# First placing in halves, the last sequence's halves side by side, and the clearing transfers three in a row behind the maxima's

## The chip, the cores and the metric

The kernel runs on one core of one Trainium2 chip. The metric is the device time of one execution in microseconds (us); less is better. TensorE (PE) multiplies matrices and loads its weights (PEld), VectorE (DVE), ScalarE (ACT) and GpSimd (POOL) work on tiles, and SyncE (SP) does little but begin DMA transfers. ACT and POOL begin some as well. Each engine takes its instructions in the order in which the program gives them; engines wait for each other with semaphores.

## The reference

The input is x, 16 sequences of 256 tokens with 128 features. Three blocks follow one another: a plain attention, and two layers of attention and a mixture of experts.

```python
x = x + layernorm(attn(layernorm(x)))          # 16 heads of 8, causal
h = x                                           # the sandwich: 2 layers
for l in range(2):
    h = h + attn(ln1(h), wq[l], wk[l], wv[l], wo[l])     # 16 heads of 8, causal
    moe = token_moe if l == 0 else seq_moe
    h = h + moe(ln2(h), ...)                    # 8 experts, 128 -> 512 -> 128, the best 2
x = x + layernorm(h)

def token_moe(h):   # each token goes to its own two experts
    cw = weights of the two largest of (h @ gw + gb), softmax over them
    return sum_e (gelu(h @ w1[e] + b1[e]) @ w2[e] + b2[e]) * cw[..., e]
def seq_moe(h):     # the two experts are chosen once per sequence, by the mean over its tokens
    ...
```

## The kernel before, in words

**A written order.** The kernel is a list of steps: `plan.put(slot, fn, phase)` notes a step, and at the end all are sorted by slot, phase (EARLY, MAIN, LATE) and order of noting, and written out (`Plan`, L352). Nothing is rearranged afterwards, so the order in a slot is the order in every engine's queue. A sequence of the attentions takes `NT` = 6 slots. Slots below 0 are the start. The plain attention has slots 0 to 95, layer 0's attention the 96 after it; layer 1's comes after the experts of layer 0.

**An attention.** Sequences go in pairs. `plan_pair` normalizes both, transposes them (`to_hT`, ACT L648) and projects q and k for all heads into PSUM (`project`, tile pp, L403). The values are split in a high part (`high`, ACT L410) and a low one (`low`, DVE L415), both in one tile hl, which has a single buffer, for q and k together. `place(k, n)` (L424) moves hl into the rows that TensorE reads: eight transfers of 256 KB for a pair, four for each sequence, from 128 partitions of hl to every eighth partition of `qk_rows[i + k]`. There are four such row tiles in turn. Their fixed rows are set once by `clear` (L169), a cast over half of the tile; the two casts of tile 0 stand at the head of ACT's queue, and those of tile 1 at slot -14. All placings are begun on SP but for two of each sequence of the first pair, which ACT begins.

`plan_sequence` then makes scores twice. A first pass (L299, with the causal mask by L276) finds the maxima of each row (DVE, mx). They are transposed, split in high and low (`high_max`, `low_max`) and sent to two more rows of qk_rows as mhi and mlo (SP, L508) at slot 3 of each group of six, EARLY. The second pass (L320) computes the scores less their maxima in the product itself, and ACT takes the exponential (pT, L324). L339 weights the values. The result is brought into order by small transfers on SP: sums and y (L522, L523), inv and r (L528, L534). POOL multiplies (y, L541), PE projects (po, L546). In the plain attention, POOL adds the input xr, which SP has loaded again (an, L636), and SP stores the sum (x, L637).

**The order on SP.** In the slots of a pair whose placings are due it is: mhi, mlo, store of x, four placings, inv, a clearing transfer, four placings, loads of xr (and for some pairs x), a clearing transfer, two r, sums, y, a clearing transfer. In the other half of the pair's twelve slots there are no placings: mhi, mlo, store of x, inv, clearing transfer, xr, clearing transfer, two r, sums, y, clearing transfer.

**Clearing.** Layer 0's experts read their tokens from x_rows, sorted by expert, and leave results in y_rows; both are DRAM arrays with room for incomplete tiles. SP writes zeros over them first, in 88 transfers of 256 KB from one zero tile (L1307), one at every even slot: 68 for x_rows, 20 for y_rows.

**Experts of layer 0.** POOL scatters the tokens' rows to x_rows (L883); tiles of 256 rows go through `plan_tokens` and their results to y_rows (`store` of a tile, POOL L1176). Tokens come in two parts, `q` = 0 and 1. Layer 1 begins with gathers (POOL L756), two for each block of 128 tokens, which must follow the stores that they read. The gathers of sequence 0 carry dependences on the stores noted so far, up to `NA_T + NB_T`. The store of the last of them (q = 1, m = `NB_T - 1` = 13) is written after the first two gathers.

**The end.** In layer 1 a sequence's expert products are added to z (L1237 and after), normalized and added to x. For the last sequence, `halves` does it for 128 tokens at a time: add (L1254), statistics, root on POOL (L248, L249), scaling and the last addition on DVE (L253, L1262), and the store on SP or ACT (L1265). Other sequences have `store` (L1288): POOL adds and then begins the output's transfer (L1290).

Of the kernel before, what the change touches and what calls it, by code (L numbers as in the profile page):

```python
# [75 lines left out]
def sandwich_kernel(  # L76
# [107 lines left out]

    nc.scalar.activation(hs[:, 0:1], nhalf[:, 0:1], AF.Exp)
    clear(nc.scalar.copy, 0, 0)
    clear(nc.scalar.copy, 0, 1)
    ones = const.tile([P, P], F32, name="ones")
    before = const.tile([P, P], F32, name="before")
    euler = const.tile([P, 1], F32, name="euler")  # L190
# [2 lines left out]
    def start_steps(plan):  # L193


        def loads():
            for b in range(2, 4):
                x0[b] = load_x(b, "x0", 6)
            nc.sync.dma_start(row, rows.partition_broadcast(P))
            nc.scalar.dma_start(wvo_sb[:, 0], wvo[0])  # L200

        def late_loads():
            for a in range(1, 3):
                nc.scalar.dma_start(wqk_sb[:, a], wqk[a])
                nc.scalar.dma_start(wvo_sb[:, a], wvo[a])
            nc.scalar.dma_start(gw_sb, gw)

        def rest():
            nc.gpsimd.memset(ones, 1.0)
            nc.gpsimd.affine_select(  # L210
                out=before, in_=ones, compare_op=ALU.is_gt, fill=0.0, base=0, pattern=[[1, P]],
                channel_multiplier=-1,
            )
            nc.gpsimd.memset(euler, math.e)
            nc.gpsimd.memset(zeros, 0.0)

        plan.put(-34, loads)
        plan.put(-14, lambda: clear(nc.scalar.copy, 1, 0), MAIN)
        plan.put(-14, lambda: clear(nc.vector.tensor_copy, 1, 1), MAIN)
        plan.put(-31, lambda: make_mask(0))  # L220
        plan.put(-31, make_pick)
        plan.put(-16, lambda: make_mask(1))
        plan.put(-34, late_loads)
        plan.put(-15, lambda: make_va(va[0]))
        for i in range(2, 4):
            for h in range(2):
                slot = (-8 + 2 * h, -4)[i - 2]
                plan.put(slot, lambda i=i, h=h: clear(nc.scalar.copy, i, h))
        plan.put(-8, lambda: make_va(va[1]))
        plan.put(-8, rest)  # L230
# [148 lines left out]
    def plan_pair(plan, i, a, sources, applied, hT_of, done=None):  # L379
# [40 lines left out]
        def place(k, n):  # L420

            q, kk = n // 2, 2 + n % 2
            eng = nc.scalar if i == 0 and n > 1 else nc.sync
            eng.dma_start(  # L424
                qk_rows[(i + k) % NQ][n : P : 8].bitcast(F32),
                st["hl"][:, q : kk + 1 : kk - q, k],
            )

        def values():
# [41 lines left out]
        plan.put(t, lambda: high(0), EARLY)  # L471
        plan.put(t, lambda: low(0))
        for n in range(4):
            plan.put(t + (n // 2 if i else 0), lambda n=n: place(0, n), (LATE, EARLY)[n // 2 if i else 0])
            plan.put(t + 2 + n // 2, lambda n=n: place(1, n), (LATE, EARLY)[n // 2])
        plan.put(s0 - 2, values)
        plan.put(s0 - 1, to_va, EARLY)
# [270 lines left out]
    def plan_combine(plan, s, b, pace, adds):  # L748


        st = {}

        def gather(i):
            if i == 0:
                st["y"] = work.tile([P, 4, D], F32, tag="yg", name=f"yg_{b}")
            get = nc.gpsimd.indirect_dma_start(  # L756
                st["y"][:, i], None, y_rows,
                bass.IndirectOffsetOnAxis(ap=ix_y[:, 2 * b + i // 2, i % 2 : i % 2 + 1], axis=0),
            ).ins

            if i == 0 and b in (0, BA):
                for store in stores[: NA_T + NB_T] if b == 0 else stores[NA_T + NB_T :]:
                    tc.add_manual_dep(get, store.name, SYNC)
            apart_from(get, "y")

        def add(i):
            zt = z[b][:, i // 2]
            nc.vector.scalar_tensor_tensor(
                zt, st["y"][:, i], w_tok2[:, 2 * b + i // 2, i % 2 : i % 2 + 1], zt,
                ALU.mult, ALU.add,  # L770
            )

        for i in range(4):
            plan.put(s + i // pace, lambda i=i: gather(i))
            plan.put(adds[i // 2], lambda i=i: add(i))
# [338 lines left out]
    def plan_tokens(plan, s, q):  # L1114

        x_blocks = x_rows.rearrange("(c i p) d -> c p i d", i=2, p=P)
        y_blocks = y_rows.rearrange("(c i p) d -> c p i d", i=2, p=P)
        spare = {}

        def room(m):  # L1120


            if m == 2:
                parts = work.tile([P, 8, 2, D], F32, tag="hl", name="x_hl", bufs=1)
                spare.update({2 + i: parts[:, i] for i in range(8)})
            if m == 10:
                parts = work.tile([P, 4, D], F32, tag="yg", name="x_yg")
                spare.update({m + i: parts[:, 2 * i : 2 * i + 2] for i in range(2)})
            if m == 12:
                spare[m] = work.tile([P, 4, D], F32, tag="xn", name="x_xn", bufs=1)[:, 0:2]  # L1130
            return spare.get(m)

        def unit(m):
            tag = f"t{q}_{m}"

            st = {}

            def fetch():
                if q:
                    load()  # L1140
                return nc.sync.value_load(ix_tile[q][0:1, m, 0:1], min_val=0, max_val=E - 1)

            def load():
                eng = nc.sync if q else nc.gpsimd
                c = eng.value_load(ix_tile[q][0:1, m, 1:2], min_val=0, max_val=BLOCKS - 1)
                st["xt"] = room(m) if q == 0 else None
                if st["xt"] is None:
                    st["xt"] = work.tile([P, 2, D], F32, tag="xr", name=f"xt_{tag}", bufs=2)
                get = eng.dma_start(st["xt"], x_blocks[bass.ds(c, 1)].squeeze(0)).ins
                for put in puts[seen[0] :]:  # L1150
                    tc.add_manual_dep(get, put.name, SYNC)
                seen[0] = len(puts)

            if q == 0:
                plan.put(s - 5 + m // 2, load, MAIN)

            def turn():

                st["pt"] = transposed(
                    [st["xt"][:, i] for i in range(2)], tag, "p" if q == 0 or m < NB_T else "m"  # L1160
                )

            def affine():
                st["h"] = work.tile([P, T], F32, tag="r", name=f"ht_{tag}")
                nc.scalar.activation(  # L1165
                    st["h"], st["pt"], AF.Identity,
                    bias=vec[:, C_LN2B : C_LN2B + 1], scale=vec[:, C_LN2W : C_LN2W + 1],
                )

            def done(po, b2):  # L1170
                y = work.tile([P, 2, D], F32, tag="ao", name=f"y_{tag}")
                nc.vector.tensor_tensor(y, po, b2.unsqueeze(1).to_broadcast([P, 2, D]), ALU.add)  # L1172
                st["y"] = y

            def store():
                store = nc.gpsimd.dma_start(y_blocks[NA_T * q + m], st["y"]).ins  # L1176
                stores.append(store)
                apart_from(store, "y")

            plan_expert(plan, s + 2 * m, tag, w_tok, fetch, lambda: st["h"], done)  # L1180
            plan.put(s + 2 * m + 5, store, EARLY)
            plan.put(s + 2 * m - 1, turn, MAIN)
            plan.put(s + 2 * m, affine, EARLY)

        for m in range(TILES_OF[q]):
            unit(m)
# [36 lines left out]
    def plan_seq(plan, s):  # L1223

        for b in range(B):
# [3 lines left out]
            def unit(b, k):  # L1229
# [19 lines left out]
                def halves(pos, b2):  # L1249

                    o = work.tile([P, 2, D], F32, tag="an", name="o_last")
                    for i, po in enumerate(pos):
                        zi = z[b][:, i : i + 1]
                        nc.vector.scalar_tensor_tensor(  # L1254
                            zi, po, we[:, b, k : k + 1], zi, ALU.mult, ALU.add
                        )
                        mv = moments(2, f"last_{i}")[:, 0:1]
                        stats(mv, zi, f"last_{i}")
                        rs = small.tile([P, 2], F32, tag="rs2", name=f"rs_last_{i}")[:, 0:1]
                        root(rs, mv)  # L1260
                        scaled(nc.vector, o[:, i : i + 1], zi, mv, rs)
                        nc.vector.tensor_tensor(  # L1262
                            o[:, i : i + 1], o[:, i : i + 1], out_st["x"][:, i : i + 1], ALU.add
                        )
# [22 lines left out]

            def store(b=b, st=out_st):  # L1288
                nc.gpsimd.tensor_tensor(st["o"], st["o"], st["x"], ALU.add)  # L1289
                nc.gpsimd.dma_start(out[b].rearrange("(i p) d -> p i d", p=P), st["o"])  # L1290

            t = s + 4 * b + 6
            plan.put(t - 4, load)
# [6 lines left out]
    start_steps(plan)  # L1300
    attention_0(plan)

    n = 0
    for t in (x_rows, y_rows):
        fill = t.rearrange("(c p r) d -> c p (r d)", p=P, r=4)
        for c in range(fill.shape[0]):
            plan.put(2 * n, lambda fill=fill, c=c: nc.sync.dma_start(fill[c], zeros))  # L1307
            n += 1
    layer_attention(plan, 0, B, finish_tok)

# [77 lines left out]
```

## Time and profile before

| what | value |
|---|---|
| time, three runs | 1017.8, 1020.77, 1027.81 us; median 1020.77 |
| profiled execution, its own time | 1017.52 us |
| its span (first to last instruction or transfer) | 1015.5 us |
| mean granted TensorE clock | 0.964 of full |
| busy: PE / DVE / ACT / POOL | 923.1 / 674.6 / 568.0 / 610.9 us |
| DMA moved | 163.64 MB, mean 161 GB/s |
| clearing transfers begun | x_rows from 43.6 to 350.7 us, y_rows from 353.1 to 440.8 us |

In a line of the profile, L is the line of the kernel, "a<-b" the written and the read tile, and the bracket at the end says how long the engine had stood idle before the instruction, and what ended that, as far as the semaphores tell. "SPq", "ACTq" lines are the beginnings of transfers. The list of waits sums such idle times: us in total, times, longest. The profile is of one execution, and sums are made against its own time.

### The profile page before, as it was taken

What the parts mean: (1) busy time and instruction counts of PE and PEld (TensorE: products, weight loads), DVE (VectorE), ACT (ScalarE), POOL (GpSimd) and SP (SyncE); (2) the same over time, 40 slices, a digit from 0 to 9 for tenths busy, and PEclk for the clock granted to TensorE, in tenths of its full rate; (3) what the DMA queues carried; (4) which work ended last, traced back from release to release, by engine and by line L of the source; (5) the groups of instructions that cost most, each with busy time, mean ns of one, the idle gap of its engine ahead of it and who ended that gap; (6) DMA issues with size and microseconds to landing.
All of it is one profiled execution on the core that took longest, in us unless ns stands there. A gap on an engine that the chain in (4) does not pass through costs nothing. (4 is left out here: it accounts for less than half of the span.)

```text
span 1015.5 us, 29356 instructions
## 1 busy us (share of the span) xinstructions
PE 923.1 (91%) x11148; PEld 721.6 (71%) x11148; DVE 674.6 (66%) x1614; ACT 568.0 (56%) x903; POOL 610.9 (60%) x1028
## 2 busy tenths in 40 slices
PE   3799889999999999998889999889999999999996
PEld 1566666666667777775788898766676677689996
DVE  3668778888788888885433413468899988445433
ACT  3565556666566666565344555345666666754442
POOL 7114666667766477658675127658688643366655
PEclk8799999999999999998799999899999999999999
DMA  6657677777877765542656787935565556256773
GB/s 162 136 121 174 169 179 188 182 188 192 191 178 173 170 168 155 166 132 71 198 166 190 218 235 235 242 91 119 125 128 116 106 113 144 67 151 197 203 202 106
DMA packets 143900, 163.64 MB, mean 161 GB/s; under 512 B 26928, under 2 KB 109872, under 8 KB 143760
## 3 DMA queue, kind: packets, MB, share of 16 engines
q1 hardware_dynamic: 133920, 142.41, 57.2%
q0 software_dynamic: 7312, 17.18, 5.6%
q10 hardware_dynamic: 2528, 2.18, 1.0%
q8 instruction: 88, 1.44, 0.6%
q14 instruction: 52, 0.43, 0.1%
HBM read 65.38 MB, written 37.36 MB: 101 GB/s over the span
## 5 line engine op out<-in xcount | busy, mean ns | idle before, releaser
L302 DVE TENSOR_REDUCE mx<-s 128x4 f32<-128x1024 f32 (+1 forms) x288 | 350.6, 1218 | 94.2 <-PE s L299 89.8
L324 ACT ACTIVATE pT<-s 128x1024 f32<-128x1024 f32 x288 | 294.4, 1023 | 164.4 <-PE s L320 160.3
L276 PEld LDWEIGHTS <-pick 64*128 64x128 bf16 x2304 | 78.1, 95 | 144.6 <-issue 122.1
L299 PE MATMUL s<-qk_rows 62*128 62x128 f32 (+1 forms) x1536 | 160.4, 306 | 11.0 <-DMA qk_rows<-hl 11.0
L320 PE MATMUL s<-qk_rows 64*128 64x128 f32 (+1 forms) x1536 | 158.4, 305 | 9.1 <-DMA qk_rows<-mlo 9.1
L339 PE MATMUL av<-pT,va 128*32 128x256 f32 (+1 forms) x3072 | 156.3, 333 | 0.0
L299 PEld LDWEIGHTS s<-qk_rows 62*128 62x128 f32 x1536 | 114.2, 194 | 13.6 <-issue 11.6
L320 PEld LDWEIGHTS s<-qk_rows 64*128 64x128 f32 x1536 | 112.3, 193 | 12.9 <-DMA qk_rows<-mhi 11.6
L276 PE MATMUL s<-mask_q,pick 64*128 64x128 bf16 (+1 forms) x1152 | 95.0, 243 | 18.8 <-DVE mx L302 14.5
L1083 ACT ACTIVATE gs_t<-ph_t,w_t 128x256 f32<-128x256 f32 x156 | 65.3, 470 | 71.5 <-PE ph_t L1079 67.0
L276 PE MATMUL s<-mask_k,pick 64*128 64x128 bf16 (+1 forms) x1152 | 94.2, 242 | 11.6 <-ACT pT L324 9.4
L339 PEld LDWEIGHTS av<-pT,va 128*32 128x32 f32 x3072 | 79.7, 110 | 33.3 <-issue 1.1
L1083 ACT ACTIVATE gs_s<-ph_s,w_s 128x256 f32<-128x256 f32 x128 | 52.7, 470 | 59.4 <-issue 57.3
L1093 PE MATMUL pe_t<-w_t,gs_t 128*128 128x128 f32 x624 | 80.4, 284 | 2.1 <-DVE y_t L1172 2.1
L1079 PE MATMUL ph_t<-ht_t,w_t 128*128 128x256 f32 x312 | 79.2, 398 | 1.7 <-ACT ht_t L1165 1.2
L883 POOL DMA_INDIRECT x_rows<-zn,ix_tok x64 | 65.1, 1017 | 25.5 <-issue 14.8
L1093 PEld LDWEIGHTS pe_t<-w_t,gs_t 128*128 128x128 f32 x624 | 76.2, 199 | 3.5 <-DVE y_t L1172 2.6
L756 POOL DMA_INDIRECT yg<-y_rows,ix_y x64 | 64.3, 1004 | 13.0 <-issue 12.7
L1172 DVE TENSOR_TENSOR y_t<-pe_t,w_t 128x256 f32<-128x256 f32 x39 | 16.5, 422 | 81.0 <-PE pe_t L1093 72.7
L1079 PEld LDWEIGHTS ph_t<-ht_t,w_t 128*128 128x128 f32 x312 | 58.7, 199 | 10.9 <-DVE mx L302 1.6
L1176 POOL DMA_DIRECT2D y_rows<-y_t x39 | 28.9, 742 | 60.6 <-DVE y_t L1172 48.4
L1093 PE MATMUL pe_s<-w_s,gs_s 128*128 128x128 f32 x512 | 62.8, 276 | 0.6 <-issue 0.6
(205 smaller groups left out, 1505.8 us busy)
## 6 DMA issues: line engine op xcount, KB each, us to landing
qk_rows<-hl SPq DMA_DIRECT2D x188, 256.0 KB
x_rows<-zeros SPq DMA_DIRECT2D x68, 256.0 KB
w_t<-in_w_tok SPq DMA_DIRECT2D x39, 320.0 KB
w_s<-in_w_seq SPq DMA_DIRECT2D x32, 320.0 KB
w_t<-in_w_tok SPq DMA_DIRECT2D x39, 258.0 KB
w_s<-in_w_seq SPq DMA_DIRECT2D x32, 258.0 KB
y<-at SPq DMA_DIRECT2D x48, 128.0 KB
r<-inv SPq DMA_DIRECT2D x96, 64.0 KB
```

The costliest lines, as they stand in the source:

```text
L276: nc.tensor.matmul(s[:, a, :, o + 64 * c : o + 64 * c + 64], pick[h, c], masks[m][h, 0:nj], start=(c == 0), stop=False, skip_group_check=True,
L299: nc.tensor.matmul(s[:, a, j], qs, ks, start=False, stop=(j == nj - 1), skip_group_check=True)
L302: nc.vector.tensor_reduce(mx[:, 0 if u is None else 1, :, j0 : j0 + nj], s, AX.X, ALU.max)
L320: nc.tensor.matmul(s[:, a, j], ks, qs, start=False, stop=(j == nj - 1), skip_group_check=True)
L324: nc.scalar.activation(pT, sc, AF.Exp, scale=SCALE)
L339: nc.tensor.matmul(o[:, P:] if u is None else o, v[:, i, 8 * par + 4 * a + jj % 4], p[:, a, j], start=(c not in first), stop=False, skip_g ...
L756: get = nc.gpsimd.indirect_dma_start(st["y"][:, i], None, y_rows, bass.IndirectOffsetOnAxis(ap=ix_y[:, 2 * b + i // 2, i % 2 : i % 2 + 1], ...
L883: put = nc.gpsimd.indirect_dma_start(x_rows, bass.IndirectOffsetOnAxis(ap=ix_tok[:, 4 * g + i, k : k + 1], axis=0), zns[2 * g + i // 2][:, ...
L1079: nc.tensor.matmul(p, w1[:, f * P : (f + 1) * P], h_of(), start=True, stop=True)
L1083: nc.scalar.activation(st["gs"][:, f], p, AF.Gelu, bias=b1[:, f : f + 1])
L1093: nc.tensor.matmul(po[:, i] if last is None else st["po"][i][:, 0], st["gs"][:, f, i * P : (i + 1) * P], st["w2"][0][:, f], start=(f == 0) ...
L1176: store = nc.gpsimd.dma_start(y_blocks[NA_T * q + m], st["y"]).ins
```

## The change

1. `clear(0, 1)`, a cast on ACT, moves from the head of the queue to slot -21, behind hT's copy.
2. The placings of the first sequence become eight transfers of 128 KB, one half of the 256 tokens each: on SP n = 0, 1 and on ACT n = 2, 3, the first halves before the second ones. The placings of the second sequence, four of 256 KB, are all begun on SP.
3. The clearing transfers go to slots 3, 4 and 5 of each group of six, instead of 0, 2 and 4. On SP, the half of the pair with placings becomes: mhi, mlo, store of x, two placings, clearing, two placings, inv, clearing, two placings, clearing, two placings, xr (x), two r, sums, y. The half without: mhi, mlo, store of x, clearing, inv, two clearings, xr, two r, sums, y. The numbers per group and the total stay.
4. The store of token tile 13 of part 1 is written one slot earlier, ahead of the first two gathers, which now carry the dependence on it. Asserts say that all stores and scatters have been noted; they emit nothing.
5. `halves` first runs addition, statistics and root of both halves and then scaling, addition and store of both.
6. The output of sequence 14 is begun on SP instead of POOL.

TensorE's instructions and their order are the same.

```diff
     clear(nc.scalar.copy, 0, 0)
-    clear(nc.scalar.copy, 0, 1)
...
         plan.put(-34, loads)
+        plan.put(-21, lambda: clear(nc.scalar.copy, 0, 1))
...
         def place(k, n):
 
             q, kk = n // 2, 2 + n % 2
-            eng = nc.scalar if i == 0 and n > 1 else nc.sync
-            eng.dma_start(
-                qk_rows[(i + k) % NQ][n : P : 8].bitcast(F32),
-                st["hl"][:, q : kk + 1 : kk - q, k],
+            if i + k:
+                nc.sync.dma_start(
+                    qk_rows[(i + k) % NQ][n : P : 8].bitcast(F32),
+                    st["hl"][:, q : kk + 1 : kk - q, k],
+                )
+
+        def place_first(n, half):
+
+            q, kk = n // 2, 2 + n % 2
+            t = slice(half * P, half * P + P)
+            (nc.sync if n < 2 else nc.scalar).dma_start(
+                qk_rows[0][n : P : 8, :, :, t].rearrange("p j w t -> p (j w) t").bitcast(F32),
+                st["hl"][:, q : kk + 1 : kk - q, 0, t],
             )
...
         for n in range(4):
-            plan.put(t + (n // 2 if i else 0), lambda n=n: place(0, n), (LATE, EARLY)[n // 2 if i else 0])
+            if i:
+                plan.put(t + n // 2, lambda n=n: place(0, n), (LATE, EARLY)[n // 2])
+            else:
+                for half in range(2):
+                    plan.put(t + half, lambda n=n, half=half: place_first(n, half), LATE - 2 * half)
...
-            plan.put(s + 2 * m + 5, store, EARLY)
+            plan.put(s + 2 * m + (4 if q and m == NB_T - 1 else 5), store, EARLY)
...
                     o = work.tile([P, 2, D], F32, tag="an", name="o_last")
+                    zi, mv, rs = [], [], []
                     for i, po in enumerate(pos):
-                        zi = z[b][:, i : i + 1]
...
-                        stats(mv, zi, f"last_{i}")
-                        rs = small.tile([P, 2], F32, tag="rs2", name=f"rs_last_{i}")[:, 0:1]
-                        root(rs, mv)
-                        scaled(nc.vector, o[:, i : i + 1], zi, mv, rs)
...
+                        stats(mv[i], zi[i], f"last_{i}")
...
+                        root(rs[i], mv[i])
+                    for i in range(2):
+                        scaled(nc.vector, o[:, i : i + 1], zi[i], mv[i], rs[i])
...
                 nc.gpsimd.tensor_tensor(st["o"], st["o"], st["x"], ALU.add)
-                nc.gpsimd.dma_start(out[b].rearrange("(i p) d -> p i d", p=P), st["o"])
+                (nc.sync if b == B - 2 else nc.gpsimd).dma_start(
+                    out[b].rearrange("(i p) d -> p i d", p=P), st["o"]
+                )
...
         for c in range(fill.shape[0]):
-            plan.put(2 * n, lambda fill=fill, c=c: nc.sync.dma_start(fill[c], zeros))
+            slot = NT * (n // 3) + (NT - LEAD + 1) % NT + n % 3
+            plan.put(slot, lambda fill=fill, c=c: nc.sync.dma_start(fill[c], zeros))
             n += 1
```

More of the change, by code (lines that the diff above doesn't have):

```diff
@@ L761, in gather @@
             if i == 0 and b in (0, BA):
+                assert len(stores) >= (NA_T + NB_T if b == 0 else NTILE)
                 for store in stores[: NA_T + NB_T] if b == 0 else stores[NA_T + NB_T :]:
@@ L1149, in load @@
                 get = eng.dma_start(st["xt"], x_blocks[bass.ds(c, 1)].squeeze(0)).ins
+                if m == 0:
+                    assert len(puts) == (4 * B if q else 4 * BA)
                 for put in puts[seen[0] :]:
@@ L1251, in halves @@
                     o = work.tile([P, 2, D], F32, tag="an", name="o_last")
+                    zi, mv, rs = [], [], []
                     for i, po in enumerate(pos):
-                        zi = z[b][:, i : i + 1]
+                        zi.append(z[b][:, i : i + 1])
                         nc.vector.scalar_tensor_tensor(
-                            zi, po, we[:, b, k : k + 1], zi, ALU.mult, ALU.add
+                            zi[i], po, we[:, b, k : k + 1], zi[i], ALU.mult, ALU.add
                         )
-                        mv = moments(2, f"last_{i}")[:, 0:1]
-                        stats(mv, zi, f"last_{i}")
-                        rs = small.tile([P, 2], F32, tag="rs2", name=f"rs_last_{i}")[:, 0:1]
-                        root(rs, mv)
-                        scaled(nc.vector, o[:, i : i + 1], zi, mv, rs)
+                        mv.append(moments(2, f"last_{i}")[:, 0:1])
+                        stats(mv[i], zi[i], f"last_{i}")
+                        rs.append(
+                            small.tile([P, 2], F32, tag="rs2", name=f"rs_last_{i}")[:, 0:1]
+                        )
+                        root(rs[i], mv[i])
+                    for i in range(2):
+                        scaled(nc.vector, o[:, i : i + 1], zi[i], mv[i], rs[i])
                         nc.vector.tensor_tensor(
@@ L1289, in store @@
                 nc.gpsimd.tensor_tensor(st["o"], st["o"], st["x"], ALU.add)
-                nc.gpsimd.dma_start(out[b].rearrange("(i p) d -> p i d", p=P), st["o"])
+                (nc.sync if b == B - 2 else nc.gpsimd).dma_start(
+                    out[b].rearrange("(i p) d -> p i d", p=P), st["o"]
+                )
             t = s + 4 * b + 6
```

## The prediction

> **What bounds the kernel now.** I read the page first: TensorE is busy for 923.1 of 1015.5 us, so an edit pays only where TensorE stands still. Then the list of waits, for where it does.
>
> ```profile
> PE s L299 <- DMA qk_rows<-hl: 11.0, 2, 8.4
> ...
> PE s L320 <- DMA qk_rows<-mlo: 9.1, 10, 1.8
> ```
>
> The first row is mostly the start: 8.41 us for the first placing. The second is the maxima's transfers, once per pair of sequences in the first two attentions; the largest is 1.8, most are 0.5 to 0.6. The change aims at both. The DMA queue's timeline for one pair shows what stands around the fills; columns: start, duration, queue, line, tile.
>
> ```profile
> 177.66 2.63 SPq L424 DMA_DIRECT2D qk_rows<-hl  x4
> 180.38 0.58 SPq L528 DMA_DIRECT2D inv<-sums  x1
> 181.01 0.99 SPq L1307 DMA_DIRECT2D x_rows<-zeros  x1
> 182.09 3.71 SPq L424 DMA_DIRECT2D qk_rows<-hl  x4
> 185.85 0.62 SPq L116 DMA_DIRECT2D xr<-in_x  x1
> ...
> 192.38 0.56 SPq L508 DMA_DIRECT2D qk_rows<-mhi  x1
> ```
>
> Eight placings and one fill pass here. The trace has the first placing's landing at 181.06, the eighth's at 192.32 and that of xr's load at 192.66. mhi, computed by 187.1, is issued 0.06 after the eighth landing: the queue's transfers use eight semaphores in turn, and it takes the eighth placing's. The DMA view of 177 to 196 us, 40 slices of 0.475 us, says what that time is:
>
> ```profile
> DMA  0161889999999999999999999999999895111802
> GB/s 22 35 235 41 160 209 369 233 192 179 183 183 179 179 179 261 343 360 226 201 203 192 188 198 183 197 185 203 244 346 359 253 365 209 65 47 37 274 0 35
> ```
>
> The engines are full from the first placing to the last: this is throughput. The timeline at its end shows who hangs on it:
>
> ```profile
> 192.50 0.69 ACT L410 ACTIVATE hl<-pp,vec 128x512 fp32r<-128x512 f32 x1 [1.59 <-DMA y<-at]
> ...
> 192.80 0.73 POOL L636 TENSOR_TENSOR an<-xr,an 128x256 f32<-128x256 f32 x1 [3.75 <-DMA xr<-in_x]
> ...
> 194.16 0.40 PE L276 MATMUL s<-mask_k,pick 64*128 64x256 bf16 x4 [0.44 <-ACT pT L324]
> ...
> 195.16 0.66 PE L320 MATMUL s<-qk_rows 64*128 64x128 f32 x8 [0.61 <-DMA qk_rows<-mlo]
> ...
> 196.96 0.71 PE L546 MATMUL po<-wvo_sb,y 128*128 128x128 f32 x4 [0.53 <-POOL y L541]
> ```
>
> hl has one buffer, so ACT writes the next one only when all eight placings have read it: 192.50, 0.18 after the eighth landing (the view names another transfer). The exponential behind it on ACT makes TensorE wait 0.44. xr is needed by POOL's addition, behind which y, and so po, wait 0.53. I looked at the same place in every pair: hl starts 0.15 to 0.20 us after the eighth landing at 81, 109, 138, 165, 192, 219, 245, 273 and 301 us (nine pairs); at 327 there is 0.3 us of slack, later 1.6 to 3.9. This part is thus bound by TensorE and by this stream almost equally.
>
> **The fills.** Still three per sequence. Before, one lay between first placing and xr, one behind xr, one behind y. Now, written order on SP: maxima, x, two placings, fill, two placings, inv, fill, two placings, fill, two placings, xr. So two fills of 256 KB more lie ahead of the eighth placing and of xr, though the maxima have none ahead of them, and take the semaphores of the sixth and seventh placing. In the sequence without placings the three stand ahead of xr too, but there the load at 195.60 lands at 198.67 and POOL's addition comes at about 204: covered by 5 us (bare, it would cost a fill's 0.8 each).
>
> What does a fill cost in a full stream? Low end: 128 packets of 2 KB at 85 ns over 16 engines, 0.68 us. The four slices around 185 us run at 261 to 360 GB/s: 256 KB at 350 is 0.75. High end: from the fourth landing (185.17) to the fifth (188.37) are 3.20 us; less one placing step of 1.36, 1.84 for inv and fill; inv alone takes about 0.35 in layer 1's streams, which leaves 1.5. The same stretch at 151 us gives 0.58. I take 0.8, as three of four readings lie there. Two are d = 1.6 us (1.2 to 3.0). Nine pairs lose d less 0.15 slack, 13.0; the pair at 327 1.3; later ones nothing: **+14.4 us**. The mlo wait of 0.6 goes, but it lies behind the late hl on the same path, and po waits for xr's full delay anyway: nothing is won there. Bounds: if engines absorb a fill beside placings at 0.2 each, the maxima's gain survives and the sum is about -3; at 1.5 each it is +28.
>
> A later stall has a second price, the clock.
>
> ```profile
> 274.10:277.50 3.40, 1.96 (x22) 1.39 (x22) 3.31 (x7) 1.26 (x2) 3.21 (x6) 1.00 0.52 165
> 277.50:280.90 3.40, 3.40 (x32) 2.29 (x34) 2.07 (x3) 1.02 (x1) 2.90 (x4) 0.50 0.34 121
> ```
>
> Columns after the stretch: length, busy PE, PE loads, DVE, ACT, POOL, granted clock, DMA share, GB/s. 1.44 us of idle TensorE in 3.4 us, and the next 3.4 us ran at 0.50: up to 1.7 us of work lost. **The Trainium skill**, "TensorE: Matmul & The Clock Gate" (HAM oscillation), gives as its abstract rule no idle gaps above about 3.4 us. By that, stalls of 2 us cost no clock, +0; by this row, where no single gap was over 0.7, they can. I follow the row. A pair has some 1.6 us of idle around 195 us now and about 3 after, so perhaps two or three of nine pairs more than today's two are hit: **+4** (0 to +12).
>
> **The start.** One clearing cast leaves the head of ACT's queue:
>
> ```profile
> 8.18 1.89 ACT L169 CAST qk_rows<-fixed 128x2048 fp32r<-128x2048 f32 x1
> ...
> 9.98 0.58 ACT L648 COPY hT<-pt_i 128x512 f32<-128x512 f32 x1
> ```
>
> The transposes were done at 8.24, so hT, the projections, hl and the first placing come 1.7 us earlier. The cast now follows hT, in the 2.16 us in which ACT waits for the projection: hidden (1.9 if not). The placings become eight halves; the first scores need half 0, 512 KB, where they now wait for 1 MB, landing from 18.65 to 23.13. Here **the Trainium skill** speaks against the edit: "DMA: Bandwidth & Descriptors" (Rules for kernel authors) says not to bother splitting a transfer in disjoint halves, as both use the same 16 engines. For the whole that would be right: it gives the 1.7 alone. But half 0 stands first, so about half of the 8.0 us from first issue to last landing suffices: first scores near 20 rather than 23.26. Runs of 512 B cost more engine time per byte (27 ns a packet unloaded against 46 for 1 KB here), 0.5 us or so at the tail. Behind it the placings of k (four on SP now) have to wait for the first's landings; their last moves from 28.72 to some 26 or 27, and with it the hl at 28.82 and all later work. Both prices together: **-2.9** (-1.5 to -3.5).
>
> **Store before gathers.** POOL's timeline and TensorE's, where layer 1 begins:
>
> ```profile
> 613.68 0.76 POOL L1176 DMA_DIRECT2D y_rows<-y_t  x1 [0.31 <-DVE y_t L1172]
> ```
>
> ```profile
> 630.34 0.58 PE L264 MATMUL pt_i<-ident,xn 128*128 128x128 f32 x2 [2.26 <-DVE xn L253]
> ```
>
> Two gathers (610.96, 612.30) went ahead of this store. It now precedes them, and they wait with it for y_t until 613.68: the first starts at 614.74 where the third did. Two gathers of 1.3 us each are pushed back, and with them rs_i, xn and this transpose, which TensorE already waits for by 2.26: **+2.5** (0, if other POOL work closes up, to +3.8, if a gather also waits for the store's landing).
>
> **The end.** DVE's second half waited behind the first's root, and that behind POOL's issue of the other output:
>
> ```profile
> 1007.51 0.81 POOL L1290 DMA_DIRECT2D out<-o  x1 [0.29 <-POOL o L1289]
> ...
> 1009.91 0.34 DVE L1254 SCALAR_TENSOR_TENSOR z<-pe_s,we,z 128x128 f32<-128x128 f32 x1
> ```
>
> pe_s of the second half was done at about 7.46, so z can run at 1007.6, aggregate by 8.6, the roots back to back on POOL until about 9.55, the last addition by 10.3 instead of 12.47. The output issue goes to SP, which has nothing left but the last halves' (free at this point; 0.8 if it delayed them): **-2.2** (-1.5 to -2.5). The asserts issue nothing.
>
> **Sum.** -2.9 + 14.4 + 4 + 2.5 - 2.2 = +15.8. The profiled execution took 1017.52, 3.25 below the median of 1020.77 and at the lower end of the three; 1017.5 + 15.8 = 1033.3, and leaning a little to the median: 1034.
>
> **Rivals.**
> *Intended:* the fills slip into a stream that has room, the maxima land early. About 6 of the 7.4 us of mlo waits from 84 to 303 us go, with two clock dips (-3): -2.9 - 9 + 2.5 - 2.2 = -11.6, or 1006; half of the dips remaining, 1008. For it: the list of waits, and moved bytes are equal. Against: engines full, and hl starting at the landing.
> *Fills free:* they cost the stream 0.4 for two, hl's delay eats the maxima's gain: start, end and gathers remain, 1015 to 1018. For it: layer 1's streams without fills (13.1 to 14.8 us) are hardly shorter than those here (13.7 to 14.8).
> *Heavy:* a fill costs 1.5 and the clock falls in most pairs: -2.9 + 28 + 8 + 2.5 - 2.2, about 1051.
> *The halves bring nothing* (all land together): 1.7 less is won, within any case.
> From d = 0.9 or so the whole is slower than before; that is the turning point between the cases.
>
> **Numbers.** My case 0.50 (own range 1023 to 1044), intended 0.22, fills free 0.13, heavy 0.15. About 1% (10 us) is what a measurement of this kernel tells from no change. Above 1031: heavy and some 0.7 of my case, 0.50; within 1%: fills free and the rest of mine, 0.28; faster 0.22. The range 1009 to 1051 leaves out most of the intended case and a part of the heavy one.
>
> **What would show it.** Right: pairs 28 to 29 us apart instead of 27, hl still starting on the eighth landing, that landing 16 us after the first placing's issue; mlo waits gone but TensorE waiting longer for pT, y and po; more rows of clock 0.5 in 80 to 310 us; first scores near 20; the wait before 630.34's transpose longer by 2.5; both last halves' z ahead of the first root's use. Wrong: hl starting with slack behind the landings, and pairs under 27 us: then a fill in the stream is cheap.

## The result

The changed kernel takes 1024.74 us (median of 19 runs, 1018.41 to 1030.69), the kernel before 1020.77 (19 runs, 1014.89 to 1027.81). The ratio is 1.0048, with a 95% interval of 1.0028 to 1.0068: 4.9 us slower (2.9 to 6.9). That lies in the range given, and the sign was right, but the forecast was 13 us. The question is which terms of the sum were too large. Every ratio here is of a kernel's fast runs, those within 1.5% of its fastest; in e1 these are only 11 of 22 and in e12 7 of 22, so for these two the medians of all runs are given as well.

The profiled execution of the changed kernel took 1028.65 us, 3.9 above its median, so its trace has some time that is chance. An example: from the last placing that SP begins for layer 0's attention (432.2 us before, 440.3 after) to the store of token tile 12 (609.9 and 622.2) both kernels do the same work in the same order apart from the last clearing transfers, and the second took 4.2 us longer. The trace is therefore read by places, not by its sum.

**The waits moved.** Three rows of TensorE's list of waits before, which the prediction didn't show:

```profile
PE s L276 <- DVE mx L302: 14.9, 29, 1.4
...
PE s L276 <- ACT pT L324: 9.4, 18, 0.9
...
PE po L546 <- POOL y L541: 3.3, 6, 1.1
```

The list after the change:

```profile
PE s L276 <- DVE mx L302: 23.7, 45, 1.4
PE s L276 <- ACT pT L324: 12.3, 20, 1.6
PE s L299 <- DMA qk_rows<-hl: 11.2, 6, 6.5
...
PE po L559 <- POOL y L554: 5.1, 9, 1.1
...
PE s L320 <- DMA qk_rows<-mlo: 1.7, 1, 1.7
```

The ten waits for mlo, 9.1 us before, are one, at the start. The waits of the masks for mx (+8.8), of the masks for pT (+2.9) and of po for y (+1.8) rose in their place. The wait for hl's placings at the start fell from 8.4 to 6.5, and four short ones are new: TensorE now catches up with the placings themselves in some pairs.

**One pair.** The DMA queue's timeline in the pair that the prediction showed:

```profile
178.22 1.28 SPq L424 DMA_DIRECT2D qk_rows<-hl  x2
179.55 0.60 SPq L1331 DMA_DIRECT2D x_rows<-zeros  x1
180.25 1.23 SPq L424 DMA_DIRECT2D qk_rows<-hl  x2
...
185.52 1.88 SPq L424 DMA_DIRECT2D qk_rows<-hl  x2
187.44 0.63 SPq L116 DMA_DIRECT2D xr<-in_x  x1
...
192.29 0.55 SPq L521 DMA_DIRECT2D qk_rows<-mlo  x1
```

The eighth placing lands at 193.57, 15.35 us after the first was begun, against 14.66 before. Two more clearing transfers have cost 0.7 us here, not 1.6. The engines at its end, from the timeline:

```profile
193.89 0.69 ACT L410 ACTIVATE hl<-pp,vec 128x512 fp32r<-128x512 f32 x1 [1.10 <-DMA qk_rows<-mhi]
193.91 0.73 POOL L649 TENSOR_TENSOR an<-xr,an 128x256 f32<-128x256 f32 x1 [4.31 <-DMA xr<-in_x]
...
194.67 0.30 DVE L237 BATCH_NORM_STATS2 st_z<-an 128x6 f32<-128x128 f32 x1 [1.01 <-POOL an L649]
...
196.96 0.29 PE L276 MATMUL s<-mask_q,pick 64*128 64x128 bf16 x4 [0.63 <-DVE mx L302]
...
198.07 0.71 PE L559 MATMUL po<-wvo_sb,y 128*128 128x128 f32 x4 [0.53 <-POOL y L554]
```

hl still starts 0.3 us after the eighth landing, and POOL's addition on the landing of xr. DVE stands still for that addition (1.01 us) with the next maximum behind it in its queue; the score tile is freed late, and the mask of the next scores waits 0.63. That has taken the place of mlo's 0.61.

**Over ten pairs** the streams, from the first placing's issue to the last one's landing, have a mean of 15.17 us, before 14.60; the pairs are 28.3 us apart, before 27.4 (e2, with the old order of the clearing transfers, has 28.3 too, so this distance alone says little). The granted clock stood at 0.5 for 7.3 us between 80 and 310 us, before for 6.8. What TensorE had to do between 60 and 335 us, in both kernels (columns as before: length, busy PE, PE loads, DVE, ACT, POOL, clock, DMA share, GB/s), is first the kernel before's, then the changed one's:

```profile
60.00:335.00 275.00, 258.13 (x3860) 185.31 (x3858) 219.35 (x427) 167.59 (x217) 166.48 (x260) 0.99 0.74 178
```

```profile
60.00:335.00 275.00, 251.66 (x3732) 180.40 (x3728) 213.34 (x415) 163.11 (x209) 165.21 (x258) 0.98 0.71 174
```

TensorE is idle for 16.9 us of these 275 before and for 23.3 after. This stretch, and the clock that goes with it, serves as the measure in the experiments.

**Start, store, end.** The first scores, before:

```profile
23.26 1.11 PE L299 MATMUL s<-qk_rows 62*128 62x128 f32 x8 [8.41 <-DMA qk_rows<-hl]
```

After the change, with the first exponentials' scores behind them:

```profile
19.89 1.11 PE L299 MATMUL s<-qk_rows 62*128 62x128 f32 x8 [6.52 <-DMA qk_rows<-hl]
...
40.86 1.12 PE L320 MATMUL s<-qk_rows 64*128 64x128 f32 x8 [1.71 <-DMA qk_rows<-mlo]
```

The latter were at 42.68: 3.4 us are won at the first point, and 1.8 are left at the second. At the boundary to layer 1, POOL, before:

```profile
609.94 0.71 POOL L1176 DMA_DIRECT2D y_rows<-y_t  x1 [2.94 <-DVE y_t L1172]
```

After:

```profile
625.97 0.71 POOL L1192 DMA_DIRECT2D y_rows<-y_t  x1 [2.95 <-DVE y_t L1188]
...
626.99 1.04 POOL L769 DMA_INDIRECT yg<-y_rows,ix_y  x1 [0.23 <-issue]
```

No gather is ahead of the store any more. From the store of tile 12 to layer 1's first placing are 32.96 us (622.24 to 655.20), before 30.93 (609.94 to 640.87): 2.0 more. The end:

```profile
1021.00 0.35 DVE L1271 SCALAR_TENSOR_TENSOR z<-pe_s,we,z 128x128 f32<-128x128 f32 x1
...
1023.67 0.36 ACTq L1285 DMA_DIRECT2D out<-o_last  x1
```

Before, the last store was begun here:

```profile
1012.50 0.36 ACTq L1265 DMA_DIRECT2D out<-o_last  x1
```

From TensorE's last group of products (1018.93) to the last store's issue are 4.74 us; before, 7.06 (1005.44 to 1012.50). 2.3 are won.

### The profile page after: what moved, and what is told of

It is laid out like the page before. It is cut to its first block, busy times and chain, and to the rows that moved or that the text cites. A ratio compares the mean times of both kernels' runs of the same rounds, so it can differ in the third digit from the quotient of the medians.

```text
span 1026.6 us, 29373 instructions
## 1 busy us (share of the span) xinstructions
PE 930.6 (91%) x11148; PEld 727.1 (71%) x11148; DVE 673.8 (66%) x1614; ACT 569.1 (55%) x903; POOL 612.3 (60%) x1027
## 5 line engine op out<-in xcount | busy, mean ns | idle before, releaser
L339 PE MATMUL av<-pT,va 128*32 128x256 f32 (+1 forms) x3072 | 159.5, 338 | 0.0
```

Of the source, the lines that this page charges most:

```text
L339: nc.tensor.matmul(o[:, P:] if u is None else o, v[:, i, 8 * par + 4 * a + jj % 4], p[:, a, j], start=(c not in first), stop=False, skip_g ...
```

## The experiments

They ran on four other chips, on each of which the kernel before takes 1061 to 1066 us (median) instead of 1021. Every ratio is against runs of the kernel before on the same chip, and microseconds worked out from it are that ratio times its 1061 to 1066 us. Where a part of the extra time lies is told at the end.

**The clearing transfers alone, and everything but them.** In the first, the kernel before gets part 3 of the change; in the second, the changed kernel loses it.

```diff
-            plan.put(2 * n, lambda fill=fill, c=c: nc.sync.dma_start(fill[c], zeros))
+            slot = NT * (n // 3) + (NT - LEAD + 1) % NT + n % 3
+            plan.put(slot, lambda fill=fill, c=c: nc.sync.dma_start(fill[c], zeros))
```

> The kernel before with the clearing transfers alone in their new slots. Theory A (two clearing transfers more in the placing stream delay hl and xr, at the 0.6 us each that the trace of the changed kernel shows, not 0.8, and with one or two clock dips): 4 to 10 us slower than before, nine pairs in the first attention each 0.5 to 1 us longer, mlo waits gone. Theory B (the predicted size): 14 to 18 us slower. Theory C (the maxima land early, the stream has room; what the changed kernel lost is in the store and in chance): 0 to 6 us faster.

Measured: 1.0031 (0.9998 to 1.0064), 3.3 us slower (-0.2 to 6.8); the medians of all runs, 1073.21 and 1065.07, lie 8.1 us apart, so the time alone sizes it loosely. The mean of ten streams is 14.97 us. TensorE is idle for 21.7 us of 60 to 335 us:

```profile
60.00:335.00 275.00, 253.26 (x3772) 181.37 (x3772) 215.60 (x418) 165.34 (x212) 166.31 (x260) 0.98 0.71 176
```

> The changed kernel with its clearing transfers back in the slots of before. Theory A: start -1.8, end -2.3, store before gathers +2, together 1 to 4 us faster than before. Theory C (the store costs more, some 6 us, since the stretch from 424 to 641 us grew by 6.5 in the changed kernel's trace): 1 to 4 us slower.

Measured: 1.0021 (0.9986 to 1.0056), from 1.5 us faster to 6 slower. By its time alone this leaves theory C standing, and this time and e1's make 5.5 us together, about the whole change's 4.9. Its trace speaks against it: the first exponentials' scores come at 40.35 us against 42.43 in e4, which has the old start; the end takes 4.73 us, as in the changed kernel; the stretch at the store is 35.64 us against 32.91 and 32.95 in e1 and e4, 2.7 more and not 6; and TensorE's idle time from 60 to 335 us is 16.3, as before. The sum of these, -1.7, lies just below the interval. The granted clock of that stretch was 0.95 in this execution and 0.99 in that of before, with the same order of work there.

**Which half of the pair.** The slots of one half moved, the other's left. In twelve slots of a pair, 9, 10 and 11 are the new ones among the placings, 3, 4 and 5 the new ones of the other half.

```diff
-            plan.put(2 * n, ...)
+            slot = 2 * NT * (n // 6) + (4, 6, 8, 9, 10, 11)[n % 6]    # e3: half with placings moved
+            slot = 2 * NT * (n // 6) + (0, 2, 3, 4, 5, 10)[n % 6]     # e4: the other half moved
```

> The kernel before, only the clearing transfers of the half of a pair that has placings moved to their new slots, those of the other half as before. Theory A: all of the loss is here, 4 to 10 us slower. If the loss comes from xr behind three clearing transfers in the other half: within 2 us of before.

> The kernel before, only the clearing transfers of the half of a pair without placings moved to their new slots. Theory A: within 2 us of before, since xr has 5 us of cover there. If the loss comes from xr behind three clearing transfers: 4 us slower or more.

Measured: the half with placings 1.0055 (1.0026 to 1.0085), 5.9 us slower; the other 1.0011 (0.9981 to 1.0041), with TensorE idle for 16.7 us. The intervals overlap a little, but only the first is clear of zero: the loss is among the placings, and xr behind three clearing transfers in the other half costs nothing that shows, as the 5 us of cover said.

**None and six among the placings.** The price by dose: 0, 1 (before), 3 (changed), 6.

```diff
+            slot = 2 * NT * (n // 6) + (3, 3, 4, 4, 5, 5)[n % 6]      # e5: none
+            slot = 2 * NT * (n // 6) + (9, 9, 10, 10, 11, 11)[n % 6]  # e6: six
```

> The kernel before, all six clearing transfers of a pair in the half without placings, behind its maxima; none among the placings. Theory A (two costs: clearing transfers among the placings, and ahead of the maxima): both go, streams of 14.0 to 14.4 us in the first attention and no mlo waits; 3 to 8 us faster than before, as long as xr, now behind six clearing transfers, stays within its 5 us of cover. Theory B (xr there is what costs): 5 us slower or more.

> The kernel before, all six clearing transfers of a pair among the placings, in twos where the changed kernel has one. This prices a clearing transfer in the stream: five more than before. Theory A (0.2 to 0.3 each, as the streams of the changed kernel, 0.4 to 0.6 longer with two more, say): streams of 15.6 to 16.1 us, 10 to 15 us slower than before in all. Predicted size (0.8 each): streams of 18.6 us, over 30 us slower. If they ride along: streams as before, time as before.

With none: 0.9962 (0.9934 to 0.9991), 4 us faster. With six: 1.0338 (1.0285 to 1.0391), 36 us slower. The mean streams are 14.53 and 14.63 with none (e5, e8), 14.59 to 14.74 with one (before, e2, e4, e7), 14.97 to 15.17 with three (changed, e1, e3, e11) and 16.58 us with six. So the first clearing transfer costs nothing that can be told from the spread, the next two 0.2 to 0.3 each, the last three 0.5 each. No dose costs the 0.8 that I took. The DMA view of a stream with six (188 to 207 us):

```profile
DMA  0126399999999999998979999999999999979510
GB/s 0 35 75 201 80 157 332 293 224 216 362 403 349 319 254 175 190 259 295 390 218 172 313 300 222 220 336 397 367 349 224 199 222 170 160 166 230 138 45 15
```

The busy share is full throughout, as it was before the change. But the bytes moved rise from 160 to 220 GB/s in slices with placings alone to 350 to 400 where clearing transfers run. A full busy share had not meant that no more bytes would go.

The landings say where a clearing transfer's time is given back. From one landing of SP's stream to the next, summed over a stream, as means of ten (the first placing takes 3.4 us throughout):

| clearing transfers | their own steps | seven placings | inv | stream |
|---|---|---|---|---|
| none (e5) | 0 | 10.1 | 1.0 | 14.5 |
| one (before) | 0.8 | 9.1 | 1.3 | 14.6 |
| three (e1) | 1.5 | 9.3 | 0.7 | 15.0 |
| three (changed) | 1.7 | 9.2 | 0.85 | 15.2 |
| six (e6) | 3.45 | 9.5 | 0.25 | 16.6 |

With the first one the placings' steps shorten by 1.0 in all, which pays for nearly all of it and of inv's 0.3. With more, the placings' steps shorten no further: each added transfer takes 0.35 to 0.65 more, and the step to inv gives a part of it back. Why these steps shorten isn't shown.

Yet the 36 us are more than the stream's 2.0 per pair. TensorE's stretch with six:

```profile
60.00:335.00 275.00, 242.62 (x3404) 172.58 (x3403) 194.53 (x382) 148.68 (x189) 149.83 (x234) 0.92 0.63 161
```

Two things are seen. TensorE is idle for 32.4 us of this stretch, over fewer pairs: they are 31.0 us apart instead of 27.4, so 3.7 us of idle time for each, before 1.7. And the granted clock falls to 0.92, as the prediction feared for stalls: it stood at 0.5 in seven stretches of 3.4 or 6.8 us, 44.4 us in all, each in another pair, 30.7 us or twice that after the one before. Those that begin at 117.9, 148.6 and 210.0 us follow the three longest idle times of TensorE between 60 and 335 us: 2.25, 2.04 and 1.87 us, which end at 116.0, 147.7 and 207.7. How the 36 us divide between the two isn't shown. In the changed kernel it is 0.98, with the transfers alone 0.98; with the old order 0.99, 0.95 and 0.96 were seen (before, e2, e4), with 6.8, 27.3 and 20.5 us at 0.5. At the changed kernel's stalls no fall of the clock can be told from chance.

**The store alone.**

```diff
-            plan.put(s + 2 * m + 5, store, EARLY)
+            plan.put(s + 2 * m + (4 if q and m == NB_T - 1 else 5), store, EARLY)
```

> The kernel before, only the store of token tile 13 one slot earlier, ahead of the two gathers. Theory A: 2 to 3 us slower, the gathers start behind the store, and from the store of tile 12 to layer 1's first placing are 2 to 3 us more than without. If a gather waits for the store's landing too: 4 us or more.

Measured: 1.0036 (1.0002 to 1.0070), 3.8 us slower (0.2 to 7.5). The stretch from the store of tile 12 to layer 1's first placing is 35.68 us (641.25 to 676.92), against 32.91 in the trace of e1, which has the old order: 2.8. In the twelve experiments' traces the stretch is 32.9 to 33.1 us with the old order (seven) and 35.6 to 37.4 with the new one (five). There is no sign of a wait for the landing: the first gather begins 1.0 us after the store's issue, as one did behind the store of tile 12 in the kernel before (609.94 and 610.96). In the changed kernel's trace the store lands at 629.80, when the gather of 626.99 has long begun.

**The changed kernel with no clearing transfer among the placings.** Part 3 replaced by e5's slots.

> The changed kernel, all six clearing transfers of a pair in the half without placings, behind its maxima. Theory A: what the transfers alone bring there, less 1.8 at the start and 2.3 at the end, and 2 to 3 lost at the store: 4 to 10 us faster than before.

Measured: 0.9942 (0.9916 to 0.9968), 6.2 us faster than before. Beside e5 this is 2 us more, as the traces' -1.8, +2.4 and -2.3 for start, store and end say together; but the two intervals overlap, and the times alone don't show it.

**The two paths behind the stream.** xr is loaded one slot earlier, ahead of the second sequence's placings: with the changed kernel's clearing slots, with e8's, and alone.

```diff
+            def again():
+                st["x"] = load_x(b, "xr", 2)
+            plan.put(s - 1, again, EARLY)
             plan.put(s, bias)          # no longer loads xr
```

> The kernel before with the clearing transfers in the changed kernel's slots, and the load of xr one slot earlier, so that it precedes the second sequence's four placings. It tells the two paths of a late stream apart, hl and xr. If the stream's lateness reaches TensorE through xr (addition on POOL, statistics on DVE, the next maximum): the waits for mx and for po after each pair go, and the time is 0 to 6 us below before's. If it goes through hl alone: as with the clearing transfers alone, 3 to 6 us slower than before, the waits only renamed.

> The changed kernel with all six clearing transfers of a pair in the half without placings, and the load of xr one slot earlier. If xr is a path of its own: of the 1.2 us that TensorE still waits for mx and po in each pair half or more goes, 9 to 15 us faster than before in all. If not: 6 us faster, as without it.

> The kernel before with nothing but the load of xr one slot earlier, ahead of the second sequence's four placings. If xr bound the loop in the kernel before too: the wait of po for y goes, 3 us faster or more. If its lateness was there covered by the maxima's (mlo) wait, which stays: within 2 us of before, and the gain of this load comes only once the maxima no longer stand behind a clearing transfer.

Measured: with the changed slots 0.9957 (0.9921 to 0.9994); alone 0.9918 (0.9876 to 0.9960), 8.7 us faster than before (the medians of all runs, 1056.47 and 1061.20, lie 4.7 apart); with e8's slots 0.9776 (0.9730 to 0.9821), 24 us faster. So xr was a path of its own already before the change, and I had it as the lesser one. Between the first two lies what the clearing transfers cost once xr is out of the way: about 4 us, as with xr in the way, though their intervals overlap. That speaks for a cost through hl and the placings. In the trace of e9 the waits of po between 60 and 335 us are gone, and those of the first pass for placings (0.3 to 1.0 in six pairs) remain. With both paths cleared the stretch is

```profile
60.00:335.00 275.00, 265.71 (x4054) 193.40 (x4053) 231.17 (x454) 176.23 (x230) 173.66 (x270) 1.00 0.80 184
```

9.3 us of idle time, a full clock, and pairs 25.9 us apart. That is more than the parts' sum (-8.7 and -6.2 make 15): that fits two waits that end nearly together, where taking away one leaves most of the other. Nothing here says how much of the rest is the clock's. This version beats both kernels.

**The first placing whole.** Four transfers of 256 KB instead of eight halves, all else as changed.

```diff
-                for half in range(2):
-                    plan.put(t + half, lambda n=n, half=half: place_first(n, half), LATE - 2 * half)
+                plan.put(t, lambda n=n: place_first(n), LATE)      # t = slice(0, T) in place_first
```

> The changed kernel with the first sequence placed in four whole transfers instead of eight halves. Theory A (the halves win by order[...]): first scores 1.5 to 2.5 us later than the changed kernel's 19.89. If the split brings nothing beyond the cast's move: within 0.5 us of 19.89.

```profile
22.24 1.11 PE L299 MATMUL s<-qk_rows 62*128 62x128 f32 x8 [8.28 <-DMA qk_rows<-hl]
...
41.43 1.12 PE L320 MATMUL s<-qk_rows 64*128 64x128 f32 x8 [0.95 <-DMA qk_rows<-mlo]
```

2.35 us later than the halves at the first scores, as theory A had it, but only 0.57 at the first exponentials' scores. The first difference is clear: the four traces with halves (changed, e2, e8, e10) have these scores at 19.9 to 20.6 us, the nine with the old start at 22.7 to 24.1. The second isn't: there the four range from 40.3 to 42.1 and the nine from 41.8 to 43.5. By single traces the cast has 1.2 of the 1.8 us won at the start and the halves 0.6, but the split lies within the spread. (e11 has one time, 1066.68: too little to compare.)

## Why the prediction was wrong

**What bounds the kernel: right.** hl on the eighth landing, xr behind it, TensorE and the stream almost equal. e3 and e4 put the loss where the prediction did. That mlo's wait would be won and nothing gained by it is what the lists of waits show. e5 says it most plainly, where no transfer was added among the placings: between 60 and 335 us the wait for mlo, 7.4 us before, is gone, and those for mx and po are 6.7 and 4.4, before 1.2 and 2.2.

**The size of a fill: wrong, the step that failed.** "I take 0.8, as three of four readings lie there. Two are d = 1.6 us." Measured, d is 0.4 to 0.6. The 0.8 is what the one clearing transfer's own step takes before. What failed is that I added it in full to the rest of the stream, because the engines' busy share was full: two more took 0.7 to 0.9 of their own together, and the step to inv gave about 0.5 back. But in that share a slow placing counts like a fast transfer; the GB/s row under it, 180 among placings and 340 to 360 at the one clearing transfer, showed that there was room, and I used it only to size the transfer. The reading that came nearer was the one I gave to a rival: streams without clearing transfers in layer 1 are hardly shorter. So the pairs lose about 0.5 us each, and the term is +3 to +6 (e1's time +3.3, TensorE's idle time +6.5 in the changed kernel's trace and +4.9 in e1's), not +14.4. The turning point was wrong too: I put it at d = 0.9, which counts a gain from the maxima that I had just called nothing. Without it, and without the clock, my terms cross zero at d = 0.43 (10 d - 1.65 = 2.6), and with d = 0.4 to 0.6 the change is indeed slower.

**The clock: wrong at this size.** +4 was for stalls of d = 1.6. With stalls of half a microsecond more no fall is seen (7.3 us at 0.5 against 6.8); with six clearing transfers, and streams 2 us longer, it came: 0.92. No single idle time of TensorE in that stretch was over 2.25 us, so the row was rightly preferred to the rule of the Trainium skill ("TensorE: Matmul & The Clock Gate", HAM oscillation: no idle gaps above about 3.4 us); it was applied to a stall that didn't come.

**The start: -2.9, measured -1.8**, inside its bounds. hl at 28.82 moved to 27.96 only. Half 0 did land early enough for the first scores, at 19.89; but the second sequence's placings behind the halves were begun at 19.62 as before, and the last of them landed at 27.62, where I had 26 or 27. As for the Trainium skill's advice ("DMA: Bandwidth & Descriptors", Rules for kernel authors): its row is on halves of the partitions, and mine are halves of the tokens, so it bears on them only through its reason, the shared engines. The order wins 2.35 us at the first scores, and 0.6 or less where it counts.

**The store: +2.5, measured +2.0 to 2.8.** The path is the one given as far as layer 1's first hT, which comes 2.0 us later behind the store of tile 12 (23.06 against 21.02). But the sign named for it, a longer wait of the transpose, didn't come: TensorE's idle time in the stretch grew by only 0.15 us, from 2.26 to 2.41, and its busy time by 1.9, from 28.7 to 30.55, at a granted clock of 0.95 instead of 1.00. All six traces with the store first have 0.95 there (after, e2, e7, e8, e10, e11) and all eight with the old order 1.00. So the new order also costs clock, which I had not thought of; how much of the loss that is isn't shown.

**The end: -2.2, measured -2.3**, by the mechanism given.

**The sum** with measured terms: -1.8 + 4.5 (between 3 and 6) + 2.4 - 2.3 = +2.8, within 1.3 and 4.3 by the ends; the result is +4.9 (2.9 to 6.9). The remaining two microseconds aren't placed by any run. The chances gave 0.28 to what came, within 1%.

## What to carry to other kernels

A full busy share of the DMA engines doesn't say that a further transfer costs its own duration. Look at the bytes moved in the same slices: if they rise where a transfer of the added kind runs, a part of its cost may be given back. Price it by dose, from none to several. And where two waits end nearly together, as hl's and xr's here, ask of both what stands ahead of them in the queue: the move of xr's load alone was worth 4.7 to 8.7 us, and this change as a whole lost 4.9.

## What the hardware showed that was not expected

The same kernel takes 1021 us in one set of runs and 1061 to 1066 on four other chips. The granted clock, 0.942 to 0.953 in ten of the twelve experiments' traces against 0.964 and 0.957 in those of before and after, is a part. Another is waits which these two traces don't have: in the trace of e4, ACT stands still twice for something that the profile doesn't name (ACT's waits).

```profile
ACT pT L324 <- remote: 14.3, 2, 9.9
```

TensorE's wait for pT is 37.0 us in all there, against 9.4 in the trace of before. In all twelve experiments' traces TensorE has one stall of 5 to 10 us between 479 and 523 us, where layer 0's attention ends; the traces of before and after have none above 4.5 us from 200 to 640 us. The cause is open. The kernel before ran beside each experiment, so a share that is the chip's own should be on both sides of each ratio; but no trace of it was taken there.
